# A decoder layer on one core: the PSUM bank of the row maxima joins the common pool

## The chip, the cores and the metric

The kernel runs on one core of one Trainium2 chip, as a single launch. The metric is device time in microseconds, the median of the runs. A profile of one execution gives times by engine: TensorE (PE for matmuls, PEld for weight loads), VectorE (DVE), ScalarE (ACT), GpSimd (POOL) and the queue that issues DMAs (SP).

## The reference

The layer takes `x` (4 batches of 256 rows, 512 wide) and a context (4 x 1601 x 512), all float32, and does three things, each followed by a residual and a layer norm:

```
x = layernorm(x + self_attention(x))       # attention over the 16 "d" entries of a token, small
x = layernorm(x + cross_attention(x, ctx)) # 32 query heads, 8 kv heads, head size 128
x = layernorm(x + ffn(x))                  # softmax over 64 experts, top 8, bias mix

# cross_attention
kv = concat([context, latents])            # 1601 + 256 = 1857 rows
q, k = rms_norm(latents @ Wq), rms_norm(kv @ Wk);  v = kv @ Wv
probs = softmax(q @ k.T / sqrt(128));  out = (probs @ v) @ Wo
```

Nearly all the work is in the cross attention.

## The kernel before

**Units and heads.** One kv head of one batch is a unit: 32 units, batch by batch. A unit has four query heads, so there are 128 heads `n`, with `n // 4` the unit. The 1857 key rows are 15 tiles of 128 (the last one of 65), taken in 8 pairs `p`, two tiles to a pair but for the last. Operands are split into a high and a low float16 part, and a product is three matmuls in a row (`mm3`, lines 233 to 235).

**The chain of one head.**
- `qk(n, p)`: the scores of one pair go to a PSUM tile `s` (L233 to 235). ScalarE copies it to SBUF (L490, tile `S`), and VectorE takes the running maximum over the pairs, `M` (L494 for p = 1, L496, and L499 for the short last pair).
- `qmax(n)`: VectorE reduces `M` over the two tiles of a pair to `M1`, 128 key positions by 256 queries (L506).
- `qmax_t(n)`: TensorE transposes `M1` into the PSUM tile `mt` (L516, two matmuls), VectorE reduces it to the maximum of each query row (`mq`, L517) and makes a slightly changed copy in bfloat16 (L519 `ml`, L521 `mw`).
- `qmax_b(n)`: TensorE transposes `mw`, spread over the partitions, back into the second part of the same `mt` tile (L528). It is then the row maximum along the free axis, as the subtraction needs it.
- `soft(n, c)`: in four chunks VectorE subtracts the maximum, straight from the `mt` bank (L537), ScalarE makes two exponentials (L540, L541), GpSimd the low part (L542). The bank of `mt` is free when the fourth subtraction has read it.
- `pv(n, t)`: 15 tiles of 6 matmuls accumulate the output tile `o` (L561 to 563).
- `oevac(n)`: VectorE takes the reciprocal of the row sums from `o` (L571, `rl`), ScalarE and VectorE write the scaled output as high and low part (L578, L580). `o_tr` transposes it by DMA (L593), and `wout` multiplies the four heads of a unit with Wo and adds to `y` (L608).

**Beside it** run the projections of the next unit: `kv_proj` (PSUM tile `kvp`; squares L395, V parts L403 and L404), `kv_n` (L418, L420), `kv_tr`, and `q_proj` (tile `qp`; L441, L451), with weights and keys loaded back from DRAM (`kv_load` L364). Between batches come `stage1` of the next batch (tile `p`, L184) and `stage3` of the last.

**PSUM.** There are eight banks, and each PSUM tile takes one. Pool `psu` has six, for every `s`, `kvp`, `qp`, `wo` tile and the small ones; `psm` has one, for `mt`; `psv` has one, for `o`. A tile can take a bank when all readers of the tile that had it are done.

**What sets the order.** The program gives each step a position (`at(pos, ...)`, constants in `AT`) and calls the steps sorted by it. The framework's scheduler then fixes the order on each engine when the program is built: it goes by a model of the engines' time, starts the earliest step whose inputs and buffers are there, and gives out banks as they come free. The engines work through their queues in that order. So a pool's size changes not only who waits for which bank but the order of instructions on all engines.

Of the kernel before, what the change touches and what calls it, by code (L numbers as in the profile page):

```python
# [10 lines left out]
F32 = mybir.dt.float32  # L11
# [4 lines left out]
PSUM = bass.MemoryType.PSUM  # L16
DRAM = bass.MemoryType.DRAM

P = 128
# [26 lines left out]
def tile_decoder(ctx: ExitStack, tc: tile.TileContext, x, cx, Wq1, bq1, Wk1, bk1, Wv1, bv1,  # L46
# [25 lines left out]
    pS = ctx.enter_context(tc.tile_pool(name="pS", bufs=8))  # L72
    pP = ctx.enter_context(tc.tile_pool(name="pP", bufs=5))
    dr = ctx.enter_context(tc.tile_pool(name="dr", bufs=1, space=DRAM))
    psu = ctx.enter_context(tc.tile_pool(name="psu", bufs=6, space=PSUM))
    psm = ctx.enter_context(tc.tile_pool(name="psm", bufs=1, space=PSUM))
    psv = ctx.enter_context(tc.tile_pool(name="psv", bufs=1, space=PSUM))

    def tps(name):
# [429 lines left out]
    def qmax_t(n):  # L509

        m = Mb[n]
        bank = psm.tile([P, 512], F32, tag="m", name=f"mt_{n}")
        mt = bank[:, 0:S].bitcast(BF16).rearrange("p (a i k) -> p a i k", a=2, i=NQ)
        mq = bank[:, S:S + NQ]
        for i in range(NQ):
            nc.tensor.transpose(mt[:, 0, i, :], m[:, i * P:(i + 1) * P], identb)  # L516
        nc.vector.tensor_reduce(mq, mt[:, 0], AX.X, ALU.max)  # L517
        ml = p2.tile([P, NQ], F32, tag="mq", name=f"ml_{n}")
        nc.vector.tensor_scalar(ml, mq, 1.0 - 1.0 / 128, None, ALU.mult)  # L519
        mw = p2.tile([P, NQ], BF16, tag="mw", name=f"mw_{n}")  # L520
        nc.vector.scalar_tensor_tensor(mw, mq, 1.0 + 1.0 / 128, ml, ALU.mult, ALU.max)  # L521
        Mb[n] = mt, mw
# [217 lines left out]
    for u in range(U):  # L740
# [24 lines left out]
        for g in range(G):  # L765
            n = 4 * u + g
            q = 4 * u + g * A["lqk"] if z else n
            w = A["lqkw"] if z else 1.0
            for p in range(NPAIR):
                at(q + p / NPAIR * w + 0.001, qk, n, p)  # L770
            at(q + w, qmax, n)
            at(q + w + A[z + "maxt"], qmax_t, n)
            at(q + w + A[z + "maxb"], qmax_b, n)
            for c in range(NCH):
                at(q + w + A[z + "exp"] + A[z + "exps"] * c, soft, n, c)
            for t in range(NT):
                at(q + A[z + "pv"] + t / NT, pv, n, t)
            at(q + A[z + "pv"] + A[z + "evac"], oevac, n)
            at(q + A[z + "out"], o_tr, n)
# [42 lines left out]
```

## Time and profile before

| | us |
|---|---|
| median of 3 runs | 2452.84 (2451.52 to 2457.87) |
| the profiled execution | 2452.89 |
| its span, first to last instruction | 2451.1 |
| TensorE busy | 2355.8 (96%) |
| ScalarE busy | 2079.8 (85%) |
| VectorE busy | 1930.7 (79%) |
| GpSimd busy | 1506.2 (61%) |
| mean granted TensorE clock | 0.989 |

TensorE's busy time counts matmuls from start to modelled end, and successive ones overlap: a busy TensorE is not one that streams without gaps. Lists of waits give the waiting engine and line, what ended the wait, the total in us, how often, and the longest. A releaser is taken from the semaphore that came last.

### The profile page before, as it was taken

Reading aid. Unit: us, or ns where it says so; the run is one execution under the profiler, and the core shown is the slowest. Engines: PE = TensorE matmul, PEld = TensorE weight load, DVE = VectorE, ACT = ScalarE, POOL = GpSimd, SP = SyncE. Lnnn points to the kernel's source line nnn. Section 1 sums busy time; section 2 is a strip of 40 time slices with the busy share of each in tenths; the row PEclk is TensorE's granted clock in tenths of the full one; section 3 lists DMA queues with packets and bytes.
Section 4 is the critical chain, followed back from the end, with each engine's and each line's share of the span. In section 5 each row is a group of like instructions: output and inputs, shape, how many; then the busy total and the mean of one; then the engine's idle time right before and its main releaser. Section 6 shows DMA issues by size and latency. Waiting matters only on the chain.

```text
span 2451.1 us, 65600 instructions
## 1 busy us (share of the span) xinstructions
PE 2355.8 (96%) x25424; PEld 2004.0 (82%) x25424; DVE 1930.7 (79%) x3748; ACT 2079.8 (85%) x4704; POOL 1506.2 (61%) x1334
## 2 busy tenths in 40 slices
PE   6799899999999999999999999999999999999997
PEld 5578788788888888888888788888888888888875
DVE  8788878887778887788778788788777887677775
ACT  4698889889898788898888798888898888889894
POOL 2367656676565666676665576567665665566554
PEclk9899999999999999999999999999999999999998
DMA  8836767656555556554545355555544444444310
GB/s 252 241 91 161 193 143 185 161 148 174 130 134 141 144 139 171 140 142 127 156 115 140 100 151 159 142 125 146 136 117 120 122 117 130 137 112 119 99 37 27
DMA packets 393073, 338.30 MB, mean 138 GB/s; under 512 B 318516, under 2 KB 328244, under 8 KB 384568
## 3 DMA queue, kind: packets, MB, share of 16 engines
q1 hardware_dynamic: 392760, 334.10, 50.9%
q8 instruction: 199, 3.26, 0.5%
q14 instruction: 114, 0.93, 0.1%
HBM read 219.46 MB, written 38.80 MB: 105 GB/s over the span
## 4 chain that ended last, share of the span: by engine, by line
PE 67%; ACT 6%; DVE 5%; issue 4%; POOL 2%; DMA 2%; POOLq 0%; DVEq 0%; ACTq 0%; SPq 0%
PE o L561 6%; PE o L563 6%; PE kvp L233 6%; PE o L562 6%; PE kvp L234 6%; PE kvp L235 6%; PE s L233 6%; PE s L235 6%; PE s L234 6%; PE wo L233 2%; PE wo L234 2%; PE wo L235 2%; DVE S L537 2%; ACT P L540 2%; PE qp L233 2%
## 5 line engine op out<-in xcount | busy, mean ns | idle before, releaser
L542 POOL TENSOR_TENSOR P<-S,P 128x1024 f16<-128x1024 f32 (+1 forms) x512 | 1035.6, 2032 | 502.7 <-ACT S L541 472.1
L561 PE MATMUL o<-Vh,P 128*128 128x129 f16 (+1 forms) x3840 | 693.7, 221 | 11.8 <-DVE ml L519 2.9
L563 PE MATMUL o<-Vh,P 128*128 128x129 f16 (+1 forms) x3840 | 693.8, 220 | 1.4 <-POOL P L542 1.3
L562 PE MATMUL o<-Vl,P 128*128 128x128 f16 (+1 forms) x3840 | 692.9, 219 | 0.0
L490 ACT COPY S<-s 128x512 f32<-128x512 f32 (+1 forms) x1024 | 576.1, 604 | 99.1 <-PE s L235 95.4
L540 ACT ACTIVATE P<-S,lnps 128x1024 f16<-128x1024 f32 (+1 forms) x512 | 569.6, 1126 | 57.1 <-DVE S L537 56.0
L537 DVE TENSOR_TENSOR S<-S,mt 128x1024 f32<-128x1024 f32 (+1 forms) x512 | 558.2, 1147 | 31.4 <-PE mt L528 31.1
L541 ACT ACTIVATE S<-S,lnps 128x1024 f32<-128x1024 f32 (+1 forms) x512 | 577.2, 1135 | 0.2
L233 PE MATMUL s<-QT,KT 128*128 128x256 f16 x1920 | 524.8, 274 | 27.6 <-DVE M L496 16.7
L235 PE MATMUL s<-QT,KT 128*128 128x256 f16 x1920 | 524.7, 273 | 0.0
L234 PE MATMUL s<-QT,KT 128*128 128x256 f16 x1920 | 524.7, 273 | 0.0
L496 DVE TENSOR_TENSOR M<-s,M 128x512 f32<-128x512 f32 x640 | 439.3, 686 | 98.9 <-ACT S L490 80.5
L233 PE MATMUL kvp<-wkv_back,kv 128*128 128x256 f16 (+1 forms) x1440 | 393.3, 273 | 6.2 <-DVE M L499 2.7
L561 PEld LDWEIGHTS <-P 128*128 128x128 f16 (+1 forms) x3840 | 375.7, 98 | 26.4 <-ACT S L541 4.1
L234 PE MATMUL kvp<-wkv_back,kv 128*128 128x256 f16 (+1 forms) x1440 | 393.3, 273 | 0.0
L235 PE MATMUL kvp<-wkv_back,kv 128*128 128x256 f16 (+1 forms) x1440 | 393.2, 273 | 0.0
L562 PEld LDWEIGHTS <-P 128*128 128x128 f16 (+1 forms) x3840 | 377.0, 98 | 12.9 <-issue 0.4
L563 PEld LDWEIGHTS <-P 128*128 128x128 f16 (+1 forms) x3840 | 375.4, 98 | 3.9 <-POOL P L542 2.2
L235 PEld LDWEIGHTS <-kv 128*128 128x128 f16 (+1 forms) x2040 | 201.8, 99 | 47.5
L234 PEld LDWEIGHTS <-kv 128*128 128x128 f16 (+1 forms) x2040 | 201.8, 99 | 47.6 <-issue 7.7
L233 PEld LDWEIGHTS <-kv 128*128 128x128 f16 (+1 forms) x2040 | 201.9, 99 | 44.0 <-issue 2.8
L233 PEld LDWEIGHTS <-KT 128*128 128x128 f16 x1920 | 188.1, 98 | 46.5 <-DVE M L496 11.2
(174 smaller groups left out, 4128.8 us busy)
## 6 DMA issues: line engine op xcount, KB each, us to landing
kv<-kvd SPq DMA_DIRECT2D x210, 512.0 KB, 3.7
wq_back<-wqd SPq DMA_DIRECT2D x24, 1024.0 KB, 6.1
wo_back<-wod SPq DMA_DIRECT2D x24, 1024.0 KB, 4.9
kvd<-kvm SPq DMA_DIRECT2D x28, 512.0 KB, 3.1
cst<-in_ctx_dram SPq DMA_DIRECT2D x24, 512.0 KB, 6.1
wkv_back<-wkvd SPq DMA_DIRECT2D x24, 512.0 KB, 4.6
st_q<-in_L_xattn_Wq_dram SPq DMA_DIRECT2D x16, 512.0 KB, 7.1
wqd<-wq SPq DMA_DIRECT2D x8, 1024.0 KB, 6.8
```

The lines of the kernel that those rows point to most:

```text
L233: nc.tensor.matmul(dst, ah, bh, start=start and k == 0, stop=False, skip_group_check=skip)
L234: nc.tensor.matmul(dst, ah, bl, start=False, stop=False, skip_group_check=skip)
L235: nc.tensor.matmul(dst, al, bh, start=False, stop=stop and k == n - 1, skip_group_check=skip)
L490: nc.scalar.copy(sv, ps[:, :m, :])
L496: nc.vector.tensor_tensor(Mx[n], ps, Mx[n], ALU.max)
L537: nc.vector.tensor_tensor(sv, sv, Mb[n].unsqueeze(1).broadcast_to([P, m, S]), ALU.subtract)
L540: nc.scalar.activation(pt[:, 0, :m, :], sv, AF.Exp, bias=lnps, scale=ES)
L541: nc.scalar.activation(sv, sv, AF.Exp, bias=lnps, scale=ES)
L542: nc.gpsimd.tensor_tensor(pt[:, 1, :m, :], sv, pt[:, 0, :m, :], ALU.subtract)
L561: nc.tensor.matmul(a[:, :P + 1], ph, v1[:k], start=t == 0 and i == 0, stop=False, skip_group_check=True)
L562: nc.tensor.matmul(a[:, :P], ph, v0[:k], start=False, stop=False, skip_group_check=True)
L563: nc.tensor.matmul(a[:, :P + 1], pl, v1[:k], start=False, stop=t == NT - 1 and i == NQ - 1, skip_group_check=True)
```

## The change

The pool `psm` is gone, `psu` has seven banks, and `mt` is taken from `psu` like any other tile. The computation is the same, instruction by instruction; the order is made anew when the program is built. As one line falls away, lines from 77 on count one less in the changed kernel (L516 becomes L515).

```diff
-    psu = ctx.enter_context(tc.tile_pool(name="psu", bufs=6, space=PSUM))
-    psm = ctx.enter_context(tc.tile_pool(name="psm", bufs=1, space=PSUM))
+    psu = ctx.enter_context(tc.tile_pool(name="psu", bufs=7, space=PSUM))
     psv = ctx.enter_context(tc.tile_pool(name="psv", bufs=1, space=PSUM))
...
     def qmax_t(n):
         m = Mb[n]
-        bank = psm.tile([P, 512], F32, tag="m", name=f"mt_{n}")
+        bank = psu.tile([P, 512], F32, tag="u", name=f"mt_{n}")
         mt = bank[:, 0:S].bitcast(BF16).rearrange("p (a i k) -> p a i k", a=2, i=NQ)
```

## The prediction, made before the changed kernel ran

> **What bounds the kernel now.** I read the page's busy shares first, then the busy times by stretches, then TensorE's waits, then the groups of VectorE, last the timeline around the longest wait at the row maxima. From the page, and from the windows of the span:
>
> ```profile
> span 2451.1 us, 65600 instructions
> PE 2355.8 (96%) x25424; PEld 2004.0 (82%) x25424; DVE 1930.7 (79%) x3748; ACT 2079.8 (85%) x4704; POOL 1506.2 (61%) x1334
> ...
> 0.00:100.00 100.00, 74.50 (x573) 58.80 (x574) 75.63 (x147) 57.42 (x190) 26.10 (x76) 0.98 0.83 240
> 100.00:500.00 400.00, 368.23 (x3926) 309.28 (x3924) 329.99 (x586) 348.93 (x742) 251.43 (x198) 0.97 0.63 164
> 500.00:2300.00 1800.00, 1783.28 (x19524) 1530.79 (x19522) 1419.58 (x2801) 1564.47 (x3571) 1147.95 (x1004) 1.00 0.50 135
> 2300.00:2451.00 151.00, 129.76 (x1411) 105.17 (x1408) 105.46 (x215) 108.99 (x203) 80.69 (x58) 0.93 0.16 45
> ```
>
> The second number of a window is TensorE's busy time, the last but two the granted clock. From 500 to 2300 us TensorE idles 16.7 of 1800 us: little can be won there, and every new wait is lost time. From 100 to 500 us it idles 31.8 us at a clock of 0.97. What it waits for (line of the waiting matmul, the releaser, total, times, longest):
>
> ```profile
> PE s L233 <- DVE M L496: 16.7, 19, 3.0
> ...
> PE kvp L233 <- DVE kh L420: 4.0, 3, 2.1
> ...
> PE mt L528 <- DVE mw L521: 2.9, 4, 0.9
> ...
> PE kvp L233 <- DVE M L499: 2.7, 2, 1.4
> ...
> PE mt L516 <- DVE M L506: 2.5, 2, 1.7
> ```
>
> The rows of s, kvp, qp and wo against VectorE's and ScalarE's evacuations are waits for a bank. All of that kind in the list come to 35 us, 22 of them between 100 and 500 us. The row maxima cost 2.5 us at L516 and 2.9 at L528, because there other matmuls stand between the steps. Where they don't, it looks like this, in the timeline of head 69 (start, us, engine, idle before and its releaser):
>
> ```profile
> 1370.89 0.33 PE L235 MATMUL p<-W,xT 128*128 128x384 f16 x1
> 1371.25 0.56 DVE L184 SCALAR_TENSOR_TENSOR qkv<-p,b 128x384 f32<-128x384 f32 x1 [0.73 <-PE p L235]
> 1371.73 0.41 DVE L499 TENSOR_TENSOR M<-s,M 65x256 f32<-65x256 f32 x1
> 1372.17 0.70 DVE L506 TENSOR_REDUCE M<-M 128x256 bf16<-128x512 f32 x1
> ...
> 1372.93 0.28 PE L516 MATMUL mt<-identb,M 128*128 128x128 bf16 x2 [1.71 <-DVE M L506]
> ```
>
> A matmul ends, VectorE reads its bank, and only behind that in its queue do the last maximum (L499) and M1 (L506) run, for which the next TensorE instruction waits: 1.71 us idle.
>
> **The change, part by part.** No instruction is added or removed: 128 mt tiles take a bank of the common pool instead of a bank of their own. But the scheduler places everything anew, so I compared the issue orders of both programs, with time counted in matmul work alone (0.109 us a matmul of 256 columns, 0.056 one of 128, the distance of starts in the timeline). Banks don't go round strictly: a tile gets whichever is free.
>
> *Bank waits, removed.* Where a score tile's wait is answered by the maximum of an earlier tile (L496), 94 of 378 such places had the releasing instruction within 1 us of matmul work ahead of the waiting matmul; now it is 2 of 197, and the median distance goes from 2.6 to 4.9 us. So nearly all of the 35 us goes: I take -34. Bounds: -35, and -17 if half come back because VectorE lags more than the order says. What is late next is the row maximum.
>
> *The row maxima's own wait, moved and grown.* With one bank, the mt transposes of head n stood behind the last subtraction (L537) of head n-1; now they don't, and come up earlier. The median matmul work between the last score tile of a head and its L516 falls from 6.9 to 4.6 us, the lower quartile from 6.3 to 2.1. In the trace M1 is done 5.0 us after that last score matmul (median; lower quartile 4.5), so the cover is gone for many heads. Worse, in 31 of 128 heads (28 of them the first of a unit, n a multiple of 4) the instruction directly ahead of L516 on TensorE is now the last matmul of o of head n-2, and on VectorE the reciprocal of that same o (rl, L571) stands ahead of M1 of head n. That is the shape of head 69. Before, no head has it. Queued behind the waiting transposes on TensorE are the next scores, projections and PV products, and everything that feeds on them.
>
> The groups that price it:
>
> ```profile
> L571 DVE RECIPROCAL rl<-o 128x2 f32<-128x2 f32 x128 | 20.8, 162 | 26.2 <-PE o L563 25.8
> L499 DVE TENSOR_TENSOR M<-s,M 65x256 f32<-65x256 f32 x128 | 53.6, 419 | 51.1 <-ACT S L490 45.2
> L506 DVE TENSOR_REDUCE M<-M 128x256 bf16<-128x512 f32 x128 | 89.1, 696 | 3.3
> ```
>
> Steps as in head 69, start to start: PV matmul 0.22 and 0.03 to VectorE, rl 0.13, L499 0.44 where it stands behind rl, M1 0.70, 0.06 back, less the 0.06 that TensorE streams meanwhile. M1 directly behind rl: 1.08 us, 12 heads. One L499 between: 1.52 us, 14 heads. Two instructions or more between: 3 heads at 1.9, 2 at 2.2. Sum 13 + 21 + 6 + 4 = 44 us, or 1.43 a head. Since the chain starts at TensorE's own last matmul, nothing that runs ahead elsewhere shortens it. The other price is the one measured row, 1.71 a head, 53 us. ScalarE can add to it: the copy of the last score tile (L490) often stands behind an exponential of 1.17 us and squares, so 2.4 a head (74 us) is the upper bound. I take 1.55, nearer to the chain, since rl is shorter than head 69's first step: +48.
>
> *Other short turn-rounds.* For the other heads L516 stands closer behind M1 too (within 0.2 us of matmul work in 73 heads, before in 2). L528, placed like that in 44 heads before, cost 2.9 us in all, so L516 may cost 3 more. The o tiles keep their one bank, and the work between the last matmul of one and the first of the next falls below 4 us in 26 turns instead of 8; the wait there (L561 for oh of L580) is 1.4 us now, so about 3 more. Together +6, bounds 0 and +20.
>
> *Clock.* The idle stretches from 100 to 500 us come with a clock of 0.97, worth 10 us. With the bank waits half of that goes, -5 (bounds 0 and -10). Against it, the 100 us around head 69 had 0.97, after waits of 2.1, 1.7 and 1.7 us, while single waits up to 1.4 us in 500-1300 us left 1.00; at 1.55 I add nothing, at 2.4 half of the 31 would each cost some 1.7 us (26).
>
> *The end.* The second transposes of head 127 (L528) come 3.6 us of matmul work later, just ahead of the PV products that need their result. Part is covered by waits of the last unit that are there already: +2, bounds 0 and +4.
>
> *At nothing:* the DMA orders on SP move as well, but loads of kv land in 3.7 us and stand over 16 us of matmul work ahead of their use; POOL at 61% gains cover, since the PV products that need its result (L542, L563) stand 11.7 us of matmul work behind it instead of 8.0 (median).
>
> **Two rules beside the rows.** The bank waits are 35 us of 2451. The Trainium skill (Perfetto Trace Analysis, section Identifying Performance Opportunities) says that a gap that repeats on the engine that should be saturated can mean too little PSUM for the next tile; read alone, that makes this change worth -34 - 5, or 2414 us. Its other advice there speaks against: find for each gap the semaphore that ends it. The gaps to come end at M1, which no bank shortens.
>
> **Sum.** -34 + 48 + 6 - 5 + 2 = +17. The profiled execution took 2452.89 us (span 2451.1 and 1.8 around it), the median of the runs is 2452.84, so nothing is to be converted: 2470 us.
>
> **Rivals.**
> *Faster, the other side:* the seventh bank is worth more in the first 500 us than the list of waits says. For it: TensorE idles 25.5 us of the first 100 us too, of which the list puts 13.9 on loads, which leaves 11.6, and the clock's 10 us may come back whole. With all of it, -35 - 10 - 11, and the chains at their floor of 44 with 0 for the tail and the small waits: -12, 2441 us. Against it: the waits of the first 100 us in the list are for projections and transposes of the first unit, not for banks. It decides where what is removed passes 44 + 7 = 51 us.
> *No change that can be measured:* the chains cost their floor, 44, and bank waits and clock give 34 + 10 back; both sides cancel, 2453 us. That the change doesn't do what it says is a rival with the other sign: mt keeps its bank for some 8 us of matmul work before a score tile takes it, a score tile's bank is taken again after 6, so the seventh bank may be none for the scores; then only 17 of the waits go and the sum is +34, 2487 us, inside the range.
> *Much slower:* 2.4 us a head, with half-clock stretches after half of them: -34 - 5 + 74 + 26 + 6 + 2 = +69: 2522 us. For it: M1 ends 5.0 us behind the last score matmul today. Against it: the subtractions of the head before now come earlier, so VectorE is freer at that point.
>
> **How the numbers follow.** Forecast 0.61 (with the seventh bank that is none), faster 0.13, no change 0.17, much slower 0.09. A measurement of this kernel can tell about 0.3%, 7.4 us, from no change; so slower 0.61 + 0.09 = 0.70, same 0.17, faster 0.13. The forecast's own range is 2461 (chains 44, bank waits -35, clock -5, 4 for the rest) to 2495 (31 x 2.0 = 62, bank waits -30, clock -5, tail and small waits 15). For 8 in 10 it reaches into the neighbours on both sides: 2445 to 2502.
>
> **What would show it.** Right: bank waits of s, kvp, qp and wo under 8 us in the waits list; the row of mt L516 for M (L505 after the change) at some 30 times and 40 to 60 us, longest about 2.5; TensorE's busy time unchanged, its idle time in 500-2300 us up from 17 to 50 or so, and in 100-500 us down from 32 to about 20. Wrong: L516's row under 30 us (then the chains are hidden), or the s rows still over 17 us (then banks were not the matter).

## Result and the profile after

The changed kernel takes 2534.07 us, median of 4 runs (2531.76 to 2536.53), beside 2452.18 for the kernel before on the same chip: a ratio of 1.0325, 95% interval 1.0312 to 1.0339. The forecast was 2470, range 2445 to 2502. It is slower, as forecast, but by 82 us and not by 17, and outside the range.

From the page of the changed kernel:

```profile
span 2533.7 us, 65442 instructions
PE 2378.5 (94%) x25424; PEld 2016.6 (80%) x25424; DVE 1937.1 (76%) x3748; ACT 2095.2 (83%) x4704; POOL 1511.4 (60%) x1334
```

Two of its stretches (TensorE's busy time second, granted clock last but two):

```profile
100.00:500.00 400.00, 357.21 (x3760) 301.05 (x3758) 321.76 (x569) 338.42 (x717) 241.79 (x191) 0.94 0.59 156
500.00:2300.00 1800.00, 1744.70 (x18907) 1488.03 (x18905) 1382.30 (x2719) 1530.74 (x3477) 1119.83 (x976) 0.99 0.49 132
```

From 500 to 2300 us TensorE idles 55.3 us instead of 16.7, from 100 to 500 us 42.8 instead of 31.8, and the clock there went from 0.97 to 0.94. What it waits for:

```profile
PE mt L515 <- DVE M L505: 96.6, 50, 6.7
...
PE mt L515 <- DVE bnmv L154: 4.8, 1, 4.8
...
PE kvp L232 <- DVE kh L419: 0.6, 1, 0.6
PE s L232 <- DVE M L493: 0.5, 1, 0.5
```

The waits for banks, 35 us before, are about 2 us now. In their place stands one line, L515: TensorE waits 101.4 us in 51 heads for the row maxima, before 4.2 us in 3.

Two heads show what such a wait is made of. Head 88, in the timeline (start, us, engine, what ended its idle time):

```profile
1785.58 1.20 ACT L540 ACTIVATE S<-S,lnps 128x1024 f32<-128x1024 f32 x1
1786.48 0.22 PE L562 MATMUL o<-Vh,P 65*128 65x129 f16 x1
1786.74 0.17 DVE L570 RECIPROCAL rl<-o 128x2 f32<-128x2 f32 x1 [0.70 <-PE o L562]
1787.12 0.44 ACT L489 COPY S<-s 128x256 f32<-128x256 f32 x1
1787.59 0.42 DVE L498 TENSOR_TENSOR M<-s,M 65x256 f32<-65x256 f32 x1 [0.68 <-ACT S L489]
1788.05 0.69 DVE L505 TENSOR_REDUCE M<-M 128x256 bf16<-128x512 f32 x1
1788.80 0.28 PE L515 MATMUL mt<-identb,M 128*128 128x128 bf16 x2 [2.10 <-DVE M L505]
```

It is the foreseen shape, rl ahead of the last maximum and M1. But VectorE itself stands 0.68 us, because ScalarE copies the last score tile first (L489), and that copy starts only at 1787.12, behind an exponential of 1.20 us and two squares (L440, about 0.34 us each) in ScalarE's queue. Head 84:

```profile
1707.51 0.61 DVE L419 SCALAR_TENSOR_TENSOR kh<-kvp,krk,kh 128x128 f16<-128x128 f32 x2 [1.66 <-ACT kh L417]
1708.63 0.16 DVE L570 RECIPROCAL rl<-o 128x2 f32<-128x2 f32 x1
1710.35 0.61 DVE L450 SCALAR_TENSOR_TENSOR qn<-qp,qrq,wb 128x128 f32<-128x128 f32 x2 [1.55 <-POOL qrq L443]
1711.72 0.69 DVE L505 TENSOR_REDUCE M<-M 128x256 bf16<-128x512 f32 x1
1712.46 0.39 PE L515 MATMUL mt<-identb,M 128*128 128x128 bf16 x2 [4.78 <-DVE M L505]
```

Here M1 stands behind a projection's norm (L450), and that one waits 1.55 us for GpSimd. TensorE stands 4.78 us, and the transpose then takes 0.39 us instead of 0.28: the clock has dropped too (0.50 from 1713 to 1716 us).

**Where the 82 us are.** I took the starts of all 25424 matmuls and subtracted from each distance between two starts the usual one of its shape (0.109 us for 256 columns, 0.056 for 128). What is left over the whole run is 105 us before and 188 after. Distances that are over 0.25 us too long hold 96 of it before and 155 after; the rest, 9 and 33, lies mostly in stretches in which matmuls run at half the pace. So 59 us are more idle time and 24 are clock. In the gaps alone L515 went from 4.6 to 109.8 us (this measure counts from the last start, the list from the modelled end).

**What put mt there.** In both built programs, tiles of one pool have their first use on TensorE strictly in the order in which the program asks for them: not one of 1606 tiles of the shared pool comes ahead of an earlier one. A bank may be any that is free, but the turn is fixed. As `qk(n+1, p)` has position n+1+p/8+0.001 and `qmax_t(n)` n+1.074, mt of head n has its turn behind exactly one score tile of the next head in 124 of 127 heads. The traces have the same counts. With a pool of its own it was three or four in 105 heads. TensorE works through its queue in order, and there every later tile of the pool stands behind mt's transposes, so it stands at L515 until M1 is there.

### The profile page after: what moved, and what is told of

The parts are those of the page before. It is cut to its first block, busy times and chain, and to the rows that moved or that the text cites. A ratio compares the mean times of both kernels' runs of the same rounds, so it can differ in the third digit from the quotient of the medians.

```text
span 2533.7 us, 65442 instructions
## 1 busy us (share of the span) xinstructions
PE 2378.5 (94%) x25424; PEld 2016.6 (80%) x25424; DVE 1937.1 (76%) x3748; ACT 2095.2 (83%) x4704; POOL 1511.4 (60%) x1334
## 5 line engine op out<-in xcount | busy, mean ns | idle before, releaser
L560 PE MATMUL o<-Vh,P 128*128 128x129 f16 (+1 forms) x3840 | 703.0, 220 | 8.2 <-DVE on L573 5.9
L562 PE MATMUL o<-Vh,P 128*128 128x129 f16 (+1 forms) x3840 | 702.9, 220 | 4.4 <-POOL P L541 4.4
L561 PE MATMUL o<-Vl,P 128*128 128x128 f16 (+1 forms) x3840 | 702.1, 219 | 0.0
L489 ACT COPY S<-s 128x512 f32<-128x512 f32 (+1 forms) x1024 | 570.6, 581 | 68.3 <-PE s L234 64.1
L536 DVE TENSOR_TENSOR S<-S,mt 128x1024 f32<-128x1024 f32 (+1 forms) x512 | 556.6, 1149 | 25.8 <-PE mt L527 24.7
L540 ACT ACTIVATE S<-S,lnps 128x1024 f32<-128x1024 f32 (+1 forms) x512 | 567.9, 1117 | 1.2
L232 PE MATMUL s<-QT,KT 128*128 128x256 f16 x1920 | 531.6, 277 | 1.9 <-ACT QT L464 1.0
L233 PE MATMUL s<-QT,KT 128*128 128x256 f16 x1920 | 532.0, 277 | 0.0
L234 PE MATMUL s<-QT,KT 128*128 128x256 f16 x1920 | 531.9, 277 | 0.0
L419 DVE SCALAR_TENSOR_TENSOR kh<-kvp,krk,kh 128x128 f16<-128x128 f32 (+1 forms) x480 | 146.4, 344 | 91.2 <-ACT kh L417 68.5
```

The costliest lines, as they stand in the source:

```text
L232: nc.tensor.matmul(dst, ah, bh, start=start and k == 0, stop=False, skip_group_check=skip)
L233: nc.tensor.matmul(dst, ah, bl, start=False, stop=False, skip_group_check=skip)
L234: nc.tensor.matmul(dst, al, bh, start=False, stop=stop and k == n - 1, skip_group_check=skip)
L489: nc.scalar.copy(sv, ps[:, :m, :])
L536: nc.vector.tensor_tensor(sv, sv, Mb[n].unsqueeze(1).broadcast_to([P, m, S]), ALU.subtract)
L540: nc.scalar.activation(sv, sv, AF.Exp, bias=lnps, scale=ES)
```

## Experiments

Theory A is that turn. Each run is compared with the kernel before on the same chip, 2451.8 to 2453.4 us.

**Six banks, shared.**
```diff
-psu ... bufs=7
+psu ... bufs=6      # in the changed kernel
```


> The changed kernel with psu at six banks instead of seven, one bank left unused: mt still shares. Theory A (the turn): a pool hands out banks strictly in the program's order of tiles, so the first write of mt of head n stands between the first and the second score tile of head n+1 on TensorE, and everything that takes a bank afterwards queues behind it until M1 is there. Then the seventh bank has little to do with the loss: the wait of mt at L515 stays at 85 to 120 us (101 after the change), 2530 to 2560 us. Theory B (more banks let the scores run ahead of VectorE, so M1 comes late): with six banks the loss goes, L515 under 40 us, 2450 to 2480 us.

2548.2 us, ratio 1.0391 (1.0370 to 1.0412), L515 waits 94.1 us, in this row and another of 5.8:

```profile
PE mt L515 <- DVE M L505: 88.3, 46, 7.8
```

The wait at L515 is there without the seventh bank, so it isn't the extra bank that brings it. The bank itself is worth 14 us in this order. The time alone doesn't show that the turn costs, since 21 us of bank waits have come back too (1.4 in the changed kernel); the runs with other turns below show it.

**Five banks and two apart.**
```diff
-psu ... bufs=6; psm ... bufs=1      # in the kernel before
+psu ... bufs=5; psm ... bufs=2
```


> The kernel before with psu at five banks and psm at two: mt apart, no longer bound to the subtractions of the head before, and two banks fewer for the scores than after the change. Theory A: mt floats behind 2 to 4 score tiles of the next head as before, so its wait at L516 stays under 12 us; only bank waits grow, to 40 to 80 us, 2455 to 2490 us. The step of the prediction (mt comes up early because it is no longer held by the last subtraction of the head before): the wait at L516 is over 40 us here too, 2490 us or more.

2574.6 us, ratio 1.0496 (1.0479 to 1.0514). The list of waits:

```profile
PE s L233 <- DVE M L496: 26.7, 28, 4.5
PE kvp L233 <- DVE M L496: 21.5, 7, 9.1
PE kvp L233 <- DVE kh L420: 21.2, 19, 2.2
...
PE mt L516 <- DVE M L506: 4.4, 3, 2.3
```

With a pool of its own mt hardly waits, as theory A says: 4.4 us at L516, and in 93 of 128 heads it starts behind three or four score tiles. With two banks it is no longer held by the last subtraction of the head before, which was the prediction's reason for mt's early place; that alone does not bring it up. But five banks for the rest cost far more than I had put down, 122 us. Six for scores and projections is near an edge.

**Later places: three score tiles ahead of mt.**
```diff
-AT = dict(maxt=0.074, maxb=0.18, exp=0.281, ...   # changed kernel
+AT = dict(maxt=0.26, maxb=0.3, exp=0.31, ...
```


> The changed kernel with mt's place in the program moved from 0.074 to 0.26 of a head behind the scores (second transposes 0.30, softmax 0.31): mt takes its turn behind three score tiles of the next head instead of one. Theory A: TensorE has two score tiles and what stands between them more to do before it needs M1; the wait at L515 falls from 101 us to 20 to 45 us, the bank waits stay under 8 us, 2440 to 2475 us. Theory B and the chain of the prediction (reciprocal of o ahead of M1) as the only cause: the order of the chain is gone in all but 3 heads, so a wait of 15 to 25 us, 2440 to 2455 us; if banks are what counts, no change from 2534 us.

2462.1 us, ratio 1.0038 (1.0025 to 1.0051), L515 waits 41.2 us in 17 heads, most of them in the first 500 us (26.1) and in the last unit (7.5), whose places have constants of their own. Three constants, with the pools as in the changed kernel, take back 72 of the 82 us. Two of the three move the second transposes and the exponentials along with mt; the run with two tiles ahead leaves the exponentials where they were.

**The last maximum ahead of ScalarE's copy of the same tile** (both read the tile's bank; the copy came first).
```diff
-        nc.scalar.copy(sv, ps[:, :m, :])
+        if m == 2:
+            nc.scalar.copy(sv, ps[:, :m, :])
...
+            nc.scalar.copy(sv, ps[:, :m, :])
```
The second copy stands behind the maximum of the short pair (L498), in the changed kernel.

> The changed kernel with the last maximum of a head (L498) issued ahead of ScalarE's copy of the same score tile, where before it followed the copy (both read one bank, so they take turns): M1 no longer waits for ScalarE's queue. Theory C (M1 is late because the copy of the last score tile stands behind exponentials and squares on ScalarE): the wait at L515 falls from 101 us to 40 to 60 us, 2480 to 2505 us. Theory of the prediction (the reciprocal of o ahead of M1 sets it): 90 us or more stay.

2479.2 us, ratio 1.0108 (1.0093 to 1.0123), just under the range expected. L515's waits fall from 101 to 61 us: the copy, which stands behind exponentials, holds up M1, as in head 88.

**Two, and four, score tiles ahead.**
```diff
+maxt=0.17, maxb=0.22, exp=0.281     # two
+maxt=0.4, maxb=0.48, exp=0.49       # four
```


> The changed kernel with the row-maxima steps placed so that mt takes its bank behind two score tiles of the next head (one in the changed kernel, three in the run before; counted over the heads: two in 124 of 127). Theory A (the turn: TensorE stands at L515 because no later tile may take a bank ahead of mt, so the wait is what M1 lacks of cover, 2.2 us for each score tile ahead): the L515 wait lies between the 101 us at one tile and the 41 us at three, 60 to 80 us, and the time between 2462 and 2534, at 2485 to 2510. Theory B (only the 31 heads with rl of o ahead of M1 cost, at 2.35 us each; they are 16 heads here): the wait falls by 35 us to about 66 us as well, but it sits in those 16 heads and the others together keep about 30.

> The changed kernel with mt behind four score tiles of the next head. Theory A: M1 is done ahead of L515 in nearly every head, the L515 wait falls to 5 to 20 us, of which most lies in the last unit, whose places are not moved; the time is 2440 to 2465 if the exponentials, which now start half a head later, are still in time for the PV products, and 2465 to 2490 if they are not, with new waits at the o matmuls for them. Theory B: nothing further is won against three tiles ahead, the wait stays at about 41 us and the time at 2462.

Two: 2499.1 us, ratio 1.0182 (1.0161 to 1.0203), in the range of time; L515 waits 57.1 us, slightly under its range. Four: 2471.7 us, ratio 1.0074 (1.0058 to 1.0091). Its waits:

```profile
PE s L232 <- DVE S L536: 13.6, 9, 2.7
PE kvp L232 <- DVE M L495: 9.8, 6, 3.0
PE mt L515 <- DVE M L505: 8.0, 5, 3.9
```

In these traces mt starts behind exactly one, two, three and four score tiles in 124 heads each, and the wait at L515 falls with every tile: 101, 57, 41, 8 us. Theory B, that only the heads with rl ahead of M1 cost, falls with the last step, since their number hardly changes from three tiles (3 heads) to four (1). But at four, new waits for banks come back, where I had looked for waits at o: the subtractions (L536) that free mt's bank run later, and the next scores wait for it.

**The later places with mt apart.**
```diff
+maxt=0.26, maxb=0.3, exp=0.31       # in the kernel before
```


> The kernel before (mt in a bank of its own, six in the common pool) with the later places of the run with three tiles ahead. It tells what the later places do by themselves. Theory A (the seventh bank is worth its 34 us of bank waits, the shared turn costs 41 us of wait at these places): here the L516 wait is under 6 us, the bank waits are 25 to 40 us, and the time is 2445 to 2460, level with the kernel before and up to 15 us under the shared pool at the same places. Theory C (the later places are themselves what won 72 us, whatever the pool): the time is under 2440, since bank waits and row-maxima waits both go.

2468.4 us, ratio 1.0062 (1.0050 to 1.0074), slower than either theory said. Where mt is apart, the later places lose 15 us; theory C is out. At the same places the shared pool was 6 us faster.

**Both cuts, and the parts of it.**
```diff
+maxt=0.26, maxb=0.3, exp=0.31, lmaxt=0.3, lmaxb=0.33, lexp=0.34  # last unit too
+ the last maximum first
```


> The changed kernel with mt behind three score tiles in every unit, the last one too, and the last maximum of a head issued ahead of ScalarE's copy of that tile. Theory A: both cuts add: L515 waits fall from 41 us to 10 to 20 us, bank waits stay under 6 us, and the time is 2430 to 2452, level with the kernel before or up to 0.9% under it. Theory B (what is won at L515 comes back at the next wait, the PV products' for the exponentials or the o bank): the L515 wait falls but the time stays at 2455 to 2465.

2478.8 us, ratio 1.0099 (1.0084 to 1.0115): outside what both theories gave. To find which part, the next run leaves the swap out, and the one after puts the swap alone into the kernel before:

> The changed kernel with mt behind three score tiles of the next head in every unit, the last one included; the copies and maxima in their old order. It differs from the run with three tiles ahead only in the last unit, and from the run with three tiles ahead and the last maximum first only in that swap. Theory A (each turn that is moved takes its own wait with it): the three waits at L515 in the last unit, 7.5 us, go, the rest stays, and the time is 2452 to 2460. Rival (the later places delay the exponentials of the last unit, where nothing stands beside them, so what is won at L515 is waited for at o): 2462 to 2480, and the last-unit places are what made the run with both cuts slower.

> The kernel before, its mt bank apart, with the last maximum of a head issued ahead of ScalarE's copy of that tile. Theory A (before, M1 is off the path, its wait is 2.5 us in all, so an earlier M1 wins nothing there; the copy that comes later holds its bank longer): 2450 to 2464, bank waits 35 to 45 us. Rival (M1 earlier brings the subtractions and so the whole chain of a head forward): 2438 to 2449.

Later places in every unit, without the swap: 2452.49 us, ratio 1.0002 (0.9994 to 1.0011), in theory A's range and level with the kernel before. In the last unit mt stands behind two score tiles here, not three, and the waits at L515 fall from 7.5 to 3.8 us there and don't go. So it was not the last unit's places that had made the run before slower.

```profile
PE mt L515 <- DVE M L505: 37.4, 17, 5.7
...
PE s L232 <- DVE M L495: 2.3, 5, 0.9
```

The swap in the kernel before: 2461.4 us, ratio 1.0034 (1.0021 to 1.0046), within theory A's range too. So the swap, worth 55 us in the changed kernel, where mt has its turn early, costs 9 us in the kernel before and 26 with three tiles ahead, where mt comes later. In the run with both cuts waits for banks are back: score tiles wait 9.3 us for maxima and 7.5 for subtractions, projections 5.1 for copies. Why those come later there I did not settle.

**Four ahead in the first seven units, three elsewhere.**

> The changed kernel with mt behind four score tiles in the first seven units (28 heads) and behind three in all others, the last unit included. Theory A (the number of tiles ahead has to cover what stands in VectorE's queue ahead of M1, which is more in the first 500 us, where weights and context are prepared): of the 26 us of waits at L515 in the first 500 us at three tiles, some 15 go, bank waits of 5 to 10 come back, and the time is 2443 to 2456, level with the kernel before or just under it. Rival (what is won there is lost to the banks, which mt now holds longer): 2456 to 2466.

2462.2 us, ratio 1.0039 (1.0025 to 1.0053): in the rival's range. L515 waits 17.7 instead of 37.4 us, but the score tiles wait 9.2 us for subtractions and 5.4 for copies.

**Three ahead everywhere, six banks.**

> The run with mt behind three score tiles in every unit, but with six banks in the shared pool instead of seven. It prices the seventh bank at a turn where the row maxima cost little more than they did before. Theory A (the prediction's term for bank waits was right, a seventh bank is worth 35 us where the waits for the row maxima don't hide it, and only 14 us in the changed kernel, where TensorE stood at L515 while the banks came free): bank waits of 25 to 45 us come back, and the time is 2475 to 2500. Rival (the common pool needs six banks and no more once mt has its place late in the turn): bank waits under 12 us and a time of 2455 to 2467.

2538.4 us, ratio 1.0352 (1.0335 to 1.0369), 86 us over the same with seven, and more than either theory said.

```profile
PE s L232 <- DVE kh L419: 9.9, 6, 3.0
PE kvp L232 <- DVE kh L419: 9.0, 11, 1.8
```

All bank waits together are 47 us there, with seven banks 5; waits at o are 27 instead of 9 us, those at L515 28 instead of 37. mt holds one of six banks, which leaves five for the rest, as in the run with five and two; that reading is argued, not tried apart. The seventh bank is worth 14 us at one tile ahead and 86 us at three. That banks come free while TensorE stands at L515 would explain the difference, but no run shows it by itself. The late turn needs the seventh bank: with six, it wins 10 us (2548.2 to 2538.4), with seven 82.

## Why the prediction was wrong

**The step that failed** is the row maxima's own wait. The sum has it at 48 us in 31 heads and 3 in the others; by the starts of matmuls it grew by 105. The other large miss, the clock, follows from it for the most part.

**Bank waits, -34.** Right: 35 us in the list became 2.

**The turn.** "Banks don't go round strictly: a tile gets whichever is free" is so for the bank, but not for the turn: mt's turn among the score tiles was fixed by its position, and the order of the changed program showed it before any run (one score tile ahead in 124 of 127 heads). I read the order by distances between M1 and L516, found them short, and went on to price single shapes. The question to ask first was what may pass mt in the new pool: nothing. The reason that I gave for mt's early place, that the last subtraction of the head before no longer holds it, is not it: in the run with five and two nothing holds it either, and L516 waits 4.4 us.

**The size of a wait, 48.** The 31 heads that I had counted cost 72.8 us, 2.35 a head, not 1.55. Fifteen of them did cost what the chain says, 1.46 on average (head 112: 1.47). The other sixteen cost 3.2: there rl was not the last thing that M1 waited for. "Nothing that runs ahead elsewhere shortens it" was true, but what runs ahead elsewhere lengthens it. I summed the durations of the VectorE instructions ahead of M1, not their own waits, for ScalarE's copy (0.68 us in head 88) and for ScalarE and GpSimd (1.66 and 1.55 in head 84). The argument that VectorE would be freer because the subtractions come earlier looked at its load and not at its queue.

**The other heads, 3.** Twenty heads outside the shape cost 36.9 us. I had priced them by L528, which 44 heads had close behind its producer at 2.9 us in all. But what L528 waits for (L517 to L521) is a few short steps in a row on TensorE's own result. M1 stands behind whatever the next unit's projections and the next batch's first stage have queued, copies of up to 3.2 us (L85) and scalings of up to 4.7 (L218) among them. The 3 us more that I had put down for o did not come: the list has 13 us there before and after.

**Clock, -5.** It was +24. I had put nothing on waits of 1.55 us, and rightly, but longer ones than 2.2 us were not in my sum. The rival with 2.4 us a head had the price of a stretch right: from 500 to 2300 us ten waits at L515 were followed by a half-pace stretch, eight of them at the 1.7 us assumed. That its 26 us come so near is partly luck: it had 15 such stretches in the 31 heads alone.

**The end, +2.** From the last 80 us of matmul work on, the run lost 8 us more than before, most of it at L515 in heads 123 to 125 (6.9 us), where I had looked at L528.

**Sum.** Of the distances over 0.25 us, 105 more at L515 and 33 less at banks make +72; 13 us of other gaps went, which I did not follow; the clock adds 24. Together 83; the spans differ by 82.6. The much slower rival, 2522 at a chance of 0.09, was the nearest: it had the flagged heads (74) and the clock (26), and lacked the twenty others. Against it I had put only that VectorE "is freer at that point".

**What would show it.** Bank waits under 8 us and 55 us of idle time from 500 to 2300 us came as said. L515's row came at 97 us, not 40 to 60; idle time from 100 to 500 us rose to 43 instead of falling to 20; TensorE's busy time rose by 23 us, since half-pace matmuls are busy longer (0.42 us instead of 0.27 for 256 columns, behind head 84).

The Trainium skill (Perfetto Trace Analysis, Matmul Optimizations) asks that all eight banks be in use. They were, before and after: eight banks in both kernels, 82 us apart.

## What to carry to other kernels

As this framework builds programs, a pool is also a queue: tiles that share it start in the order in which they were asked for, so a tile whose input comes late stops all that follow it, with seven banks (101 us) as with six (94). Give such a tile its own buffer, or a place in the turn behind enough work to cover its input, found in the built order (here three score tiles; two and four were worse, and even three was only level with the bank apart, and only with all seven banks). When you price a wait, follow the releaser's queue back through the waits of the instructions ahead of it, not through their durations alone.

## What the chip showed that I had not expected

A short wait can cost more than itself. Of the waits at L515 in the changed kernel between 500 and 2300 us that stand alone (distance of starts less 0.06 us), fourteen from 1.15 to 1.98 us are followed by matmuls at full pace, with 0.02 us lost over the next 7 us. Eight from 2.26 to 4.27 us lose another 1.6 to 1.7 us, and two of 4.94 and 5.42 us another 2.8 and 2.4. In single microseconds behind the 2.26 us wait of head 88:

```profile
1789.00:1790.00 1.00, 1.00 (x10) 0.74 (x8) 0.88 (x4) 1.00 (x3) 0.85 (x2) 0.90 0.07 16
1790.00:1791.00 1.00, 1.00 (x3) 0.30 (x2) 0.74 (x5) 0.70 (x2) 1.00 (x2) 0.50 0.00 0
1793.00:1794.00 1.00, 1.00 (x6) 0.44 (x5) 0.00 (x0) 0.00 (x0) 0.40 (x1) 0.90 0.02 8
```

The granted clock (last but two) goes to half about 1 us after the work has begun again, stays there for about 3.4 us, and returns. In this kernel alone it looks as if the length of the wait decided, with a step between 2.03 us (a wait at 492 us, also without loss) and 2.26. The other runs show that it does not. The wait at L515 that ends 945 us into the span is 2.37 us long both with three tiles ahead and with the last unit moved too; from 945 to 950 us the first has half clock, the second none:

```profile
945.00:950.00 5.00, 4.79 (x30) 3.69 (x31) 3.13 (x9) 4.23 (x11) 4.02 (x4) 0.66 1.03 257
945.00:950.00 5.00, 4.86 (x53) 4.45 (x54) 4.11 (x10) 5.00 (x16) 4.02 (x4) 1.00 1.05 255
```

What decides is where the wait lies. In each of the fourteen traces all half-clock stretches begin on one grid of 3.413 us, which lies differently from trace to trace, and they last one or more whole cells of it, but for the last one, which ends with the kernel. Sort TensorE's idle time between matmuls from 500 to 2300 us into the cells of that grid, over all fourteen traces. Of the cells at full clock, all 47 with 2.1 us or more of idle time are followed by a cell at half clock, three of the 8 with 2.0 to 2.1, and one of the 115 with 1.2 to 2.0. A wait of 3.34 us in the run with both cuts (it ends at 967 us) is split by a border of cells into less than 2.0 us on either side, and the clock stays at 1.00.

The Trainium skill (TensorE: Matmul & The Clock Gate, Part 1) puts the fall to half clock behind an idle window of about 3.4 us. Here 2.1 us of idle time within one cell of 3.413 us were enough; the measurement decides for this kernel. So a wait of 2.1 us or more may or may not cost another 1.7 us, by where it falls, and shorter ones hardly do unless others lie beside them.
